# Layer 3 of a graph network: the edge products with W2 on two halves of TensorE, the bias written to PSUM ahead of them

## The chip, the cores and the metric

The kernel runs on one core of a Trainium2 chip. The metric is the device time of one execution in microseconds (us). The kernel before was run ten times: its median is 5800.87 us, the runs lie between 5796.89 and 5811.82 us. One further execution was recorded by the hardware profiler.

The engines are named as in the profile: PE is TensorE (PEld its weight loads), DVE is VectorE, ACT is ScalarE, POOL is GpSimd, SP is SyncE. A core's PSUM has eight banks of 128 partitions x 512 fp32 values.

## What is computed

Four graph layers over 8,192 nodes with 32 features and 262,144 edges sorted by destination; after each layer the node features are summed with the result and normalised. The change is in layer 3, where each edge has its own small weight matrices, made by a two-layer network from 32 edge features:

```python
h = relu(edge_feat @ W1 + b1)                      # 262144 x 64
w = (h @ W2 + b2).reshape(e, 4, 8, 8)              # 262144 x 256
s, v = node_attr[:, :8], node_attr[:, 8:].reshape(n, 8, 3)
m0 = 0.25 * (einsum(s[src]*sh0, w[:,0]) + C110 * einsum(v[src], sh1, w[:,3]))
m1 = 0.25 * (einsum(s[src], sh1, w[:,1]) + einsum(v[src]*sh0, w[:,2]))
out = segment_sum([m0, m1], dst) + self-interaction
x = layernorm(x + out)
```

`sh0` and `sh1` are the four values of `edge_attr_4`. All arithmetic is fp32.

## The kernel before

Layers 0 to 2 fill the first 3,180 us or so and are untouched. Layer 3 begins at line 1031 of `raw_layers`. It takes 512 edges at a time, four tiles of 128, called a **quad**; there are NQ = 512 quads, and two consecutive quads, q even and q + 1, are called a **pair** here (256 pairs).

Order is written out by hand. Each engine has a `Flow`: `after(marks)` makes the engine's queue wait for marks, `mark(ins)` gives one; every engine executes its instructions in the order in which the loop (lines 1162 to 1246) issues them. For iteration q that order is:

- `hidden(q + 2)`, for even q (lines 1139 to 1155): PE multiplies W1 with the edge features of two quads at once, on different 32-row and 64-column parts of the array, into the lower and upper 64 partitions of PSUM bank 2 (L1146). Then ACT makes relu with the bias b1 and moves each quad's 64x512 to SBUF `hs` (L1154), one instruction for a quad. There are four such buffers, each with a 65th row of ones, set once (L1067).
- the products with W2 (L1166 to 1172): four matmuls on PE, 65 rows x 128 edges against 65 rows x 256 columns; the 65th row of `w2_s` is b2, which the row of ones adds. They write two PSUM banks (3 and 4, or 5 and 6 in turn, `w_bank`). They wait for the quad's relu and for `w_free`, the mark of DVE's last read of these banks two quads earlier. Each fp32 matmul is two passes in the trace, so a quad has eight weight loads and eight matmuls.
- `fetch_rows(q + 8)` (L1089): POOL waits for the products of q, then issues four indirect gathers of 128 source rows each (L508, shown as L454, where the helper stands). So POOL may run eight quads ahead. Gathers are also limited to two groups of eight under way.
- the aggregation of quad q - 4 (L1179): a one-hot matrix against the message parts `p`, 344 columns, accumulated over a pair in bank 0 or 1. It waits for DVE's work on quad q - 2.
- on DVE: `factors` of the next pair (L1105 to 1117, waits for the pair's gathered rows), pieces of earlier quads (L1193, L1198), the one-hot matrix (L588), and then the products of the PSUM weights with the gathered values (L1207, L1210, three of L1214). The last of these is the mark `quad[q]["v"]` and `w_free`.
- on DVE, every second iteration: the sums of a finished pair (L1235 to L1238) into `win`.
- eight times in the layer, when a block of 1,024 nodes is complete (L1242): `windows` adds up the block's window sums on PE in the first half of a W2 bank (L575), and `normalize` runs on DVE with Square and Sqrt on ACT (L525 to L537, ACT at L532 and L534).

Edge features and `edge_attr_4` come by SP's queue, eight quads at a time, three buffers (`fetch`).

Of the kernel before, what the change touches and what calls it, by code (L numbers as in the profile page):

```python
# [15 lines left out]
AF = mybir.ActivationFunctionType  # L16
# [5 lines left out]
P = 128  # L22
N = 8192
E = 262144
D = 32
# [178 lines left out]
def raw_layers(tc, x, a, w0, w1, b1, w2, si, m, bad):  # L204
    nc = tc.nc
    PE, V, A, G, S = (Flow(tc, e, n) for e, n in ((nc.tensor, "pe"), (nc.vector, "dve"), (nc.scalar, "act"),
                                                  (nc.gpsimd, "pool"), (nc.sync, "sp")))
    bank, arena = m["bank"], m["arena"]
    x_a, x_b, src, row, rel = (m[k] for k in ("x_a", "x_b", "src", "row", "rel"))
    ident, shift, stack, small = (m[k] for k in ("ident", "shift", "stack", "small"))  # L210
# [40 lines left out]
    cut = Carve()  # L251
# [20 lines left out]
    cut = Carve(8192)  # L272
# [279 lines left out]
    def windows(c, acc, free):  # L552

        d0 = c * LC
        todo = []
        for j in [0, 1, 2, 3, -2, -1, 4]:
            lo, hi = 0, LC
            while 4 * (d0 + lo) + j < 0:
                lo += 1
            while 4 * (d0 + hi - 1) + j >= GG:  # L560
                hi -= 1
            if lo < hi:
                todo.append((j, lo, hi))
        nw = win.shape[1] // 4
        wv = win.rearrange("p (d j) f -> p d j f", j=4)
        PE.after(*free)
        pieces = []
        for j, lo, hi in todo:
            g0 = (4 * (d0 + lo) + j) // 4 % nw
            cutat = lo + min(hi - lo, nw - g0)  # L570
            pieces.append((j, lo, cutat, g0))
            if cutat < hi:
                pieces.append((j, cutat, hi, 0))
        for n, (j, lo, hi, g0) in enumerate(pieces):
            ins = PE.e.matmul(acc[:, lo * D:hi * D].rearrange("p (d f) -> p d f", f=D),  # L575
                              shift[:, P - WS * j:2 * P - WS * j], wv[:, g0:g0 + hi - lo, j % 4, :],
                              start=(n == 0), stop=(n == len(pieces) - 1))
        return PE.mark(ins)
# [457 lines left out]
    w1_s = cut(64)  # L1036
    b1_s = cut(1)
    w2_s = cut(256)
    hs = cut(4, 512)
    ef = cut(3, 2, 512)  # L1040
    sh = cut(3, WT, 4)
    a0 = cut(2, WT, 16)
# [19 lines left out]
        c_ld.add(S.e.dma_start(w1_s[q * D:(q + 1) * D, :], w1))  # L1062
    for h in range(2):
        c_ld.add(S.e.dma_start(b1_s[64 * h:64 * h + 64], b1))
    c_in = c_ld.add(S.e.dma_start(w2_s[0:65], w2))
    for k in range(4):
        hm = V.mark(V.e.memset(hs[64:65, k], 1.0))  # L1067

    e_ld = [Landing(tc, f"ld_ef{k}") for k in range(3)]
    s_ld = [Landing(tc, f"ld_sh{k}") for k in range(3)]  # L1070
# [50 lines left out]
    fetch(2)  # L1121
    PE.after(*free)
    A.after(*free)
    A.after(c_in, hm)

    h_free = None
    w_free = [zf[0], zf[1]]
# [11 lines left out]
    def hidden(q):  # L1139

        s = q // 8
        k = s % 3
        PE.after(batch[s]["e"], quad.get(q - 1, {}).get("h", h_free))
        for h in range(2):
            r = q % 4 + h
            ins = PE.e.matmul(bank[64 * h:64 * h + 64, 2, :], w1_s[r * D:(r + 1) * D, :],  # L1146
                              ef[r * D:(r + 1) * D, k, (q % 8) // 4, :], start=True, stop=True,
                              tile_position=(r * D, 64 * h))
        pm = PE.mark(ins)
        if q % 8 == 6:  # L1150
            ef_free[k] = pm
        for h in range(2):
            A.after(pm, quad.get(q + h - 4, {}).get("w"))
            quad[q + h] = dict(h=A.mark(A.e.activation(hs[0:64, (q + h) % 4], bank[64 * h:64 * h + 64, 2, :], AF.Relu,  # L1154
                                                       bias=b1_s[64 * h:64 * h + 64])))

    for q in range(AHEAD):
        fetch_rows(q)
    factors(0)
    PE.after(c_in, *zf)  # L1160
    hidden(0)
    for q in range(NQ + LAG3 + 2):

        if q % 2 == 0 and q + 2 < NQ:
            hidden(q + 2)
        if q < NQ:  # L1166
            k, wp = w_bank()
            PE.after(quad[q]["h"], w_free[k])
            for t in range(4):
                ins = PE.e.matmul(wp[:, t, :], hs[0:65, q % 4, t * P:(t + 1) * P], w2_s[0:65], start=True, stop=True)  # L1170
            quad[q]["w"] = PE.mark(ins)
            quad[q]["k"] = k, wp
            fetch_rows(q + AHEAD)
        c = q - LAG3
        if 0 <= c < NQ:
            g = c // 2
            PE.after(quad[c + 2]["v"], agg_free[g % 2] if c % 2 == 0 else None)
            for t in range(4):
                ins = PE.e.matmul(bank[:, g % 2, 0:MW], oh[:, c % NO, t, :], p[:, c % NP, t, :],  # L1179
                                  start=(c % 2 == 0 and t == 0), stop=(c % 2 == 1 and t == 3))  # L1180
            quad[c]["a"] = PE.mark(ins)

        prev = (V.sem, V.n)
        if q % 2 == 0 and q + 2 < NQ:
            factors(q // 2 + 1)
        V.after(prev)
        if q < NQ:
            V.after(factor[q // 2])
        V.after(quad.get(q - NP, {}).get("a"))
        ins = None  # L1190
        if 0 <= q - 2 < NQ:
            c = q - 2
            ins = V.e.tensor_tensor(p[:, c % NP, :, 320:344].rearrange("p t (o m) -> p t o m", m=3),  # L1193
                                    red[:, c % 2, :, :, None].to_broadcast([P, 4, 8, 3]),
                                    sh[:, (c // 8) % 3, (c % 8) * 4:(c % 8) * 4 + 4, None, 1:4].to_broadcast([P, 4, 8, 3]),
                                    op=OP.mult)
        if 0 <= q - 1 < NQ:
            ins = V.e.tensor_reduce(red[:, (q - 1) % 2], pr[:, (q - 1) % 2].rearrange("p t (o i) -> p t o i", i=8),  # L1198
                                    AX.X, OP.add)
        if q < NQ:  # L1200
            k, wp = quad[q]["k"]
            s, u = q // 8, (q // 8) % 2
            qs = slice((q % 8) * 4, (q % 8) * 4 + 4)
            pq = p[:, q % NP]
            one_hot(oh[:, q % NO], 4 * q, 4)
            V.after(quad[q]["w"])
            V.e.tensor_tensor(pr[:, q % 2].rearrange("p t (o i) -> p t o i", i=8),  # L1207
                              wp[:, :, 128:192].rearrange("p t (o i) -> p t o i", i=8),
                              xg[:, batch[s]["xg"], qs, None, 0:8].to_broadcast([P, 4, 8, 8]), op=OP.mult)
            V.e.tensor_tensor(pq[:, :, 0:128].rearrange("p t (o k) -> p t o k", k=16),  # L1210
                              wp[:, :, 0:128].rearrange("p t (o k) -> p t o k", k=16),
                              a0[:, u, qs, None, :].to_broadcast([P, 4, 8, 16]), op=OP.mult)
            for mm in range(3):
                ins = V.e.tensor_tensor(pq[:, :, 128 + 64 * mm:192 + 64 * mm].rearrange("p t (o i) -> p t o i", i=8),  # L1214
                                        wp[:, :, 192:256].rearrange("p t (o i) -> p t o i", i=8),
                                  vm[:, u, qs, mm, None, :].to_broadcast([P, 4, 8, 8]), op=OP.mult)
        if ins is not None:
            d = V.mark(ins)
            if q < NQ + 2:
                quad.setdefault(q, {})["v"] = d  # L1220
            if q < NQ:
                w_free[k] = d
                if 4 * (q + 1) % TP == 0:
                    taken[batch[s]["xg"]][4 * (q % 8) // TP] = d
            if 0 <= q - 2 < NQ and (q - 2) % 8 == 7:
                s = (q - 2) // 8
                sh_free[s % 3] = d
                if s + 3 < NS:
                    fetch(s + 3)

        c = q - LAG3 - 1
        if 0 <= c < NQ and c % 2 == 1:
            g = c // 2
            V.after(quad[c]["a"])
            V.e.tensor_reduce(win[:, g, 0:8], bank[:, g % 2, 0:128].rearrange("p (o k) -> p o k", k=16), AX.X, OP.add)  # L1235
            rm = V.mark(V.e.tensor_reduce(r1, bank[:, g % 2, 128:320].rearrange("p (mo i) -> p mo i", i=8), AX.X, OP.add))
            V.after(rm)
            gm = V.mark(V.e.tensor_tensor(win[:, g, 8:].rearrange("p (o m) -> p o m", m=3),  # L1238
                                          bank[:, g % 2, 320:344].rearrange("p (o m) -> p o m", m=3),
                                          r1.rearrange("p (m o) -> p o m", o=8), op=OP.add))  # L1240
            agg_free[g % 2] = gm
            while done < NB // LC and ready(done) <= g + 1:  # L1242
                k, wp = w_bank()
                acc = bank[:, 3 + 2 * k, 0:LC * D]
                w_free[k] = normalize(3, done, acc, windows(done, acc, (w_free[k], gm)), z, x_a)
                done += 1


# [469 lines left out]
```

## Time and profile before

| what | value |
|---|---|
| median of ten runs | 5800.87 us |
| the profiled execution, its time | 5800.9 us |
| the profiled execution, its span from first to last instruction | 5799.2 us |
| mean granted clock of PE | 0.885 |
| PE busy, matmuls | 4739.6 us, 82% of the span, 34,726 instructions |
| DVE busy | 4409.4 us, 76% |
| POOL busy | 4148.7 us, 72% |
| ACT busy | 1888.8 us, 33% |
| layer 3, 3183.00 to 5753.79 us: busy PE / DVE / ACT / POOL | 2468.12 / 2072.19 / 355.35 / 1947.70 of 2570.79 us |
| layer 3: granted clock | 0.96 |

The page of a profile gives, for each group of instructions, the line, the engine, the operation with its shapes and count, then "busy us, mean ns of one | idle time of the engine just before them, and what ended most of it". Matmuls are pipelined, so the mean duration of one is longer than the distance between two starts. The slices of the page are 40 equal parts of the span, some 145 us each; a digit is the busy share in tenths, and for PEclk the granted clock in tenths of full speed. A timeline row has the start and the length of a run of like instructions and how many they are.

### The profile page before, as it was taken

What the parts mean: (1) busy time and instruction counts of PE and PEld (TensorE: products, weight loads), DVE (VectorE), ACT (ScalarE), POOL (GpSimd) and SP (SyncE); (2) the same over time, 40 slices, a digit from 0 to 9 for tenths busy, and PEclk for the clock granted to TensorE, in tenths of its full rate; (3) what the DMA queues carried; (4) which work ended last, traced back from release to release, by engine and by line L of the source; (5) the groups of instructions that cost most, each with busy time, mean ns of one, the idle gap of its engine ahead of it and who ended that gap; (6) DMA issues with size and microseconds to landing.
All of it is one profiled execution on the core that took longest, in us unless ns stands there. A gap on an engine that the chain in (4) does not pass through costs nothing.

```text
span 5799.2 us, 89080 instructions
## 1 busy us (share of the span) xinstructions
PE 4739.6 (82%) x34726; PEld 3373.1 (58%) x34726; DVE 4409.4 (76%) x9512; ACT 1888.8 (33%) x3061; POOL 4148.7 (72%) x4238
## 2 busy tenths in 40 slices
PE   7456777768777788744499999999999999999998
PEld 3146666666666666522255666666666666666665
DVE  4269898989989898543356788878788878788786
ACT  5255555555555555200177111111111111111110
POOL 2677777777777777777356777777777777777775
PEclk7578888999899899756599899999999999999999
DMA  9636666769789799945576111111111111111111
GB/s 346 218 107 198 193 205 225 254 227 323 243 299 313 274 346 327 346 137 186 208 272 221 26 26 30 26 30 30 26 30 26 30 30 26 30 26 30 26 30 22
DMA packets 583102, 865.29 MB, mean 149 GB/s; under 512 B 102605, under 2 KB 441614, under 8 KB 549134
## 3 DMA queue, kind: packets, MB, share of 16 engines
q1 hardware_dynamic: 448094, 782.68, 38.2%
q0 software_dynamic: 134144, 73.67, 6.6%
q8 instruction: 275, 4.51, 0.3%
q10 hardware_dynamic: 432, 3.15, 0.2%
q14 instruction: 157, 1.29, 0.1%
HBM read 454.28 MB, written 404.88 MB: 148 GB/s over the span
## 4 chain that ended last, share of the span: by engine, by line
PE 27%; POOL 10%; DMA 6%; DVE 4%; issue 4%; ACT 0%; POOLq 0%; SPq 0%; DVEq 0%
PE bank L1179 11%; POOL f_arena L454 10%; PE bank L1170 9%; DMA f_arena<-fxtab,f_src 5%; PE bank L1009 4%; PE bank L1146 2%; PE bank L575 1%; DVE f_arena L1214 1%; DMA f_arena<-famat 1%; DVE f_arena L1210 0%; DVE f_arena L588 0%; PE bank L937 0%; PE bank L715 0%; DVE f_arena L1112 0%; DVE f_arena L1207 0%
## 5 line engine op out<-in xcount | busy, mean ns | idle before, releaser
L454 POOL DMA_INDIRECT f_arena<-fytab,f_row x2048 | 1960.5, 957 | 651.7 <-issue 542.2
L454 POOL DMA_INDIRECT f_arena<-fxtab,f_src x2048 | 1950.6, 952 | 643.4 <-issue 517.5
L654 PE MATMUL bank<-f_arena 64*128 64x128 f32 x16384 | 1207.6, 305 | 402.6 <-DVE f_arena L643 269.9
L654 PEld LDWEIGHTS bank<-f_arena 64*128 64x128 f32 x16384 | 1110.4, 211 | 483.6 <-DVE f_arena L643 296.1
L1179 PE MATMUL bank<-f_arena 128*128 128x344 f32 x4096 | 1313.0, 463 | 0.0
L1170 PE MATMUL bank<-f_arena 65*128 65x256 f32 x4096 | 1021.8, 393 | 70.3 <-DVE f_arena L1214 69.9
L1154 ACT ACTIVATE f_arena<-bank,f_arena 64x512 f32<-64x512 f32 x512 | 351.1, 686 | 2117.4 <-PE bank L1146 2110.9
L1170 PEld LDWEIGHTS bank<-f_arena 65*128 65x128 f32 x4096 | 770.1, 193 | 423.5 <-DVE f_arena L1214 142.1
L1179 PEld LDWEIGHTS bank<-f_arena 128*128 128x128 f32 x4096 | 800.0, 195 | 359.1 <-issue 31.7
L658 ACT ACTIVATE f_arena<-bank 128x512 uint8<-128x512 f32 x1024 | 612.9, 599 | 847.5 <-PE bank L654 723.7
L659 ACT ACTIVATE f_arena<-bank 128x512 f32<-128x512 f32 x1024 | 610.7, 596 | 0.0
L640 DVE TENSOR_TENSOR f_arena<-bank,f_arena 128x2048 f32<-128x2048 bf16 x256 | 586.6, 2291 | 8.7
L1214 DVE TENSOR_TENSOR f_arena<-bank,f_arena 128x256 f32<-128x256 f32 x1536 | 550.6, 413 | 0.0
L845 PE MATMUL bank<-f_arena 128*128 128x96 bf16 x2048 | 151.7, 225 | 325.2 <-DVE f_arena L811 325.0
L1110 DVE TENSOR_TENSOR f_arena<-f_arena 128x192 f32<-128x192 f32 x256 | 92.1, 360 | 399.0 <-DMA f_arena<-fxtab,f_src 397.3
L715 PE MATMUL bank<-f_arena,f_x_b 128*32 128x256 f32 x4096 | 312.7, 446 | 77.1 <-DMA f_arena<-famat 59.2
L588 DVE TENSOR_TENSOR f_arena<-bank,f_rel 128x512 f32<-128x512 f32 x512 | 348.6, 681 | 0.0
L1210 DVE TENSOR_TENSOR f_arena<-bank,f_arena 128x512 f32<-128x512 f32 x512 | 348.5, 681 | 0.0
L845 PEld LDWEIGHTS bank<-f_arena 128*128 128x128 bf16 x2048 | 110.4, 108 | 408.8 <-DVE f_arena L811 324.4
L638 DVE TENSOR_TENSOR f_arena<-bank,f_arena 128x1024 f32<-128x1024 bf16 x256 | 312.0, 1219 | 18.2 <-PE bank L654 16.0
L643 DVE TENSOR_TENSOR f_arena<-f_arena,bank 128x1024 f32<-128x1024 f32 x256 | 309.6, 1210 | 0.0
L965 POOL CAST f_arena<-f_arena 128x1536 bf16<-128x1536 uint8 x64 | 169.6, 2664 | 182.0 <-DMA f_arena<-fcmat 68.3
(146 smaller groups left out, 4404.8 us busy)
## 6 DMA issues: line engine op xcount, KB each, us to landing
famat<-f_arena SPq DMA_DIRECT2D x256, 1024.0 KB
f_arena<-famat SPq DMA_DIRECT2D x256, 1024.0 KB, 12.0
fytab<-f_arena SPq DMA_DIRECT2D x64, 1024.0 KB, 11.9
fcmat<-f_arena SPq DMA_DIRECT2D x256, 256.0 KB
f_arena<-fcmat SPq DMA_DIRECT2D x16, 4096.0 KB, 14.7
f_arena<-fytab,f_row POOLq DMA_INDIRECT x2048
f_arena<-fxtab,f_src POOLq DMA_INDIRECT x2048
f_arena<-laid_ea SPq DMA_DIRECT2D x64, 512.0 KB, 3.4
```

What stands on the lines that cost most here:

```text
L454: return G.e.indirect_dma_start(out=dest, out_offset=None, in_=table, in_offset=bass.IndirectOffsetOnAxis(ap=ix, axis=0))
L588: return V.e.tensor_tensor(o, iota[:, None, :].to_broadcast([P, n, P]), rel[:, t:t + n, None].to_broadcast([P, n, P]), op=OP.is_equal)
L640: V.e.tensor_tensor(oh_l[:, b], iota2[:, None, :, 0].to_broadcast([P, 16, P]), meta_l[:, pp, k0:k0 + 16, None].to_broadcast([P, 16, P]), o ...
L654: ins = PE.e.matmul(two[:, h].rearrange("p (c s j) -> p c s j", s=64, j=4)[:, :, :, j], oh_l[hs_, b, 4 * q + j, :], oh_k[hs_, b, 4 * q + j ...
L658: A.e.activation(st_c[:, b, q], two[:, :, 0:256], AF.Copy)
L659: pair_free[u] = am = A.mark(A.e.activation(st_a[:, b, :, q].rearrange("p z h w -> p h z w"), two[:, :, 256:512].rearrange("p h (z w) -> p ...
L715: ins = PE.e.matmul(acc[q * D:(q + 1) * D, :].rearrange("p (u h j) -> p u h j", h=2, j=4), x_b[:, 8 * z + s, :], mv[:, s], start=(first an ...
L1154: quad[q + h] = dict(h=A.mark(A.e.activation(hs[0:64, (q + h) % 4], bank[64 * h:64 * h + 64, 2, :], AF.Relu, bias=b1_s[64 * h:64 * h + 64])))
L1170: ins = PE.e.matmul(wp[:, t, :], hs[0:65, q % 4, t * P:(t + 1) * P], w2_s[0:65], start=True, stop=True)
L1179: ins = PE.e.matmul(bank[:, g % 2, 0:MW], oh[:, c % NO, t, :], p[:, c % NP, t, :], start=(c % 2 == 0 and t == 0), stop=(c % 2 == 1 and t = ...
L1210: V.e.tensor_tensor(pq[:, :, 0:128].rearrange("p t (o k) -> p t o k", k=16), wp[:, :, 0:128].rearrange("p t (o k) -> p t o k", k=16), a0[: ...
L1214: ins = V.e.tensor_tensor(pq[:, :, 128 + 64 * mm:192 + 64 * mm].rearrange("p t (o i) -> p t o i", i=8), wp[:, :, 192:256].rearrange("p t ( ...
```

## The change

The products use 64 rows instead of 65, and there are two sets side by side: the relu of a pair lies in one 128x512 buffer whose lower 64 partitions hold tiles 0 and 1 of both quads and whose upper 64 hold tiles 2 and 3. W2 is loaded to both halves of the partitions. A quad's four matmuls are issued in the order 0, 2, 1, 3, alternately on the lower and upper 64 rows of the array; tiles 0 and 1 write one bank, 2 and 3 the other. The edge features are laid out on the host to match.

The bias b2 is no longer a row of the product. It is loaded to all partitions (`b2_s`), and for each quad ACT copies it, four times over, to the quad's two PSUM banks before the products (new `biases`, 128x1024); the products then accumulate (`start=False`). The copy waits for `w_free`, the products wait for the copy. So that PSUM accumulates onto values that ACT wrote, the four banks are written once by PE at the layer's beginning (new `written`), and after each use by `windows`, the second half of that bank is written by PE again. Relu is one 128x512 instruction for a pair instead of two of 64x512, and `hs` has two buffers instead of four. In the program's order ACT gets the relu of q + 2 (for even q), then the bias copy of q, then that of q + 1.

```diff
-    hs = cut(4, 512)
+    b2_s = cut(256)
+    hs = cut(2, 512)
...
-    c_in = c_ld.add(S.e.dma_start(w2_s[0:65], w2))
-    for k in range(4):
-        hm = V.mark(V.e.memset(hs[64:65, k], 1.0))
+        c_ld.add(S.e.dma_start(w2_s[64 * h:64 * h + 64], w2[0:64, :]))
+    c_in = c_ld.add(S.e.dma_start(b2_s, w2[64:65, :].to_broadcast([P, 256])))
...
-        for h in range(2):
-            A.after(pm, quad.get(q + h - 4, {}).get("w"))
-            quad[q + h] = dict(h=A.mark(A.e.activation(hs[0:64, (q + h) % 4], bank[64 * h:64 * h + 64, 2, :], AF.Relu,
-                                                       bias=b1_s[64 * h:64 * h + 64])))
+        A.after(pm, quad.get(q - 3, {}).get("w"))
+        hm = A.mark(A.e.activation(hs[:, q // 2 % 2], bank[:, 2, :], AF.Relu, bias=b1_s))
+        quad[q] = dict(h=hm)
+        quad[q + 1] = dict(h=hm)
+
+    def written(b, c0):
+
+        return PE.e.matmul(bank[:, b, c0:512].rearrange("p (r c) -> p r c", c=256), ident,
+                           b2_s[:, None, :].to_broadcast([P, 2 - c0 // 256, 256]), start=(c0 == 0), stop=True,
+                           skip_group_check=True)
+
+    def biases(k, wp):
+
+        A.after(w_free[k])
+        return A.mark(A.e.activation(wp, b2_s[:, None, :].to_broadcast([P, 4, 256]), AF.Copy))
...
     hidden(0)
+    for b in range(3, 7):
+        ins = written(b, 0)
+    w_free[:] = [PE.mark(ins)] * 2
...
             k, wp = w_bank()
-            PE.after(quad[q]["h"], w_free[k])
-            for t in range(4):
-                ins = PE.e.matmul(wp[:, t, :], hs[0:65, q % 4, t * P:(t + 1) * P], w2_s[0:65], start=True, stop=True)
+            PE.after(quad[q]["h"], biases(k, wp))
+            for t in (0, 2, 1, 3):
+                hp, c0 = slice(32 * (t & 2), 32 * (t & 2) + 64), 256 * (q % 2) + t % 2 * P
+                ins = PE.e.matmul(wp[:, t, :], hs[hp, q // 2 % 2, c0:c0 + P], w2_s[hp], start=False, stop=True,
+                                  skip_group_check=True)
...
-                w_free[k] = normalize(3, done, acc, windows(done, acc, (w_free[k], gm)), z, x_a)
+                windows(done, acc, (w_free[k], gm))
+                w_free[k] = normalize(3, done, acc, PE.mark(written(3 + 2 * k, 256)), z, x_a)
...
-    laid["ea32"] = arrays["ea32"].reshape(P, 4, 512, D).transpose(1, 3, 0, 2).reshape(P, P, 512)
+    laid["ea32"] = arrays["ea32"].reshape(P, 2, 2, 2, 256, D).transpose(1, 3, 5, 0, 2, 4).reshape(P, P, 512)
```

## The prediction

> **What bounds the kernel now.** I read the page's table of slices first, then the groups by cost, then the waits of GpSimd (POOL) in layer 3, the stretch from 3183 to 5754 us that the change touches.
>
> ```profile
> PE   7456777768777788744499999999999999999998
> POOL 2677777777777777777356777777777777777775
> PEclk7578888999899899756599899999999999999999
> ...
> L454 POOL DMA_INDIRECT f_arena<-fxtab,f_src x2048 | 1950.6, 952 | 643.4 <-issue 517.5
> L654 PE MATMUL bank<-f_arena 64*128 64x128 f32 x16384 | 1207.6, 305 | 402.6 <-DVE f_arena L643 269.9
> L1179 PE MATMUL bank<-f_arena 128*128 128x344 f32 x4096 | 1313.0, 463 | 0.0
> L1170 PE MATMUL bank<-f_arena 65*128 65x256 f32 x4096 | 1021.8, 393 | 70.3 <-DVE f_arena L1214 69.9
> ```
>
> In slices 22 to 39 PE looks full (9) and POOL only 7 tenths busy. That misleads. The waits of POOL between 3183 and 5753 us tell it otherwise (line waited for; us, times, longest):
>
> ```profile
> POOL f_arena L454 <- issue: 516.9, 1696, 0.3
> POOL f_arena L454 <- DMA f_arena<-fxtab,f_src: 55.5, 182, 0.3
> ```
>
> No gap between two of the 2,048 gathers is over 0.3 us: POOL never waits for anybody, it issues without a break. In the timeline the first starts at 3179.33 and the last at 5752.85, lasting 0.94. That is 2574.5 us, or **10.06 us for a pair of quads** (256 pairs). VectorE (DVE) agrees: in layer 3 it waits 389.5 us at L1110 for gathered rows. PE is busy, but is it late? The timeline of the stage's end, where PE works without waiting (start, us, operation):
>
> ```profile
> 5757.17 1.89 PE L1170 MATMUL bank<-f_arena 65*128 65x256 f32 x8
> ...
> 5758.90 2.48 PE L1179 MATMUL bank<-f_arena 128*128 128x344 f32 x8
> ...
> 5761.22 1.89 PE L1170 MATMUL bank<-f_arena 65*128 65x256 f32 x8
> ```
>
> Start to start, a quad's W2 products take 1.73 and its aggregation (L1179) 2.32 us. Around `hidden` I use this stretch, PE and then ScalarE (ACT):
>
> ```profile
> 4504.70 1.07 PE L1146 MATMUL bank<-f_arena 32*64 32x512 f32 x4
> 4505.71 1.99 PE L1170 MATMUL bank<-f_arena 65*128 65x256 f32 x8
> 4507.54 1.32 PE L1179 MATMUL bank<-f_arena 128*128 128x344 f32 x4
> ```
> ```profile
> 4505.83 1.40 ACT L1154 ACTIVATE f_arena<-bank,f_arena 64x512 f32<-64x512 f32 x2 [7.91 <-PE bank L1146]
> ```
>
> Hidden to products 1.01, products to aggregation 1.83; aggregation to hidden is 2.42 elsewhere (5740.30 to 5742.72). PE's pair: 2.42 + 1.01 + 1.83 + 2.32 + 1.73 = 9.31 us, 0.75 under POOL's 10.06. So the gathers bound layer 3 and PE is a close second.
>
> **The change, part by part.** Sums go against the profiled execution, 5800.9 us (span 5799.2 and 1.7 around it); the median shown is 5800.87, the same.
>
> *Products in halves.* 8 passes of 256 columns at 0.216 (1.73 / 8) become 4 steps of two passes side by side, if the halves overlap. L654 has just that shape, 64 rows on each half: 16,384 passes of 128 columns keep PE busy for 1207.6 us, 74 ns each, or 148 for 256 columns, where L1170 has 1021.8 / 4096 = 249. L654's share includes low clock; in its bursts at full clock two passes start together every 0.112 us. So 4 x 0.216 = 0.87 us for a quad where nothing precedes it, instead of 1.73; bounds 0.87 and 1.73 (no overlap). I take 0.87. By itself this frees 1.7 us of a pair on an engine that was not the bound: worth nothing.
>
> *Changes of array shape.* Before: aggregation to hidden (2.42 - 2.32 = 0.10) and hidden to products (1.01 - 4 x 512 columns two at a time, 0.86 = 0.15). After, products to aggregation and back are changes too: three more of 0.10 to 0.20 in a pair (two to an odd quad's products and back, one behind the even quad's). I take 0.15. The Trainium skill ("TensorEngine Tiling (Array Packing)", Key Properties) says that a change of tiling mode drains TensorE; without any such cost the pair's sum below would be 9.48.
>
> *Relu of two quads at once.* L1154's two of 0.70 (1.40 / 2) become one over 128 partitions, 0.70: half a relu less for ACT, which was waiting anyway.
>
> *Bias first, and where it queues.* This decides. Each quad gets a 128x1024 copy on ACT into PSUM. No row has SBUF to PSUM; bounds: L481, 128x1024 from PSUM, 1.03 us; L532 (SBUF, 128x256, 0.41) and L659 (128x512, 0.60) bound the slope and give 0.96 to 1.1. I take 1.03. Two make 2.1 us of ACT's idle 8.7 in a pair: no load problem. But the order is: PE runs `hidden(q+2)`, then the products of q, which wait for the bias of q. ACT has relu of q+2 **ahead of** that bias, and that relu waits for the very `hidden(q+2)` PE has just issued. PE cannot go on: hidden ends, 0.05 (L1146's end to L1154's start), relu 0.70, bias 1.03, 0.05 back: **1.83 us in which PE stands, once a pair**. Behind the waiting products on PE's queue lie the aggregation of q-4, the next products, and with them VectorE's turn and POOL's gather for q+8 (L1092). The odd quad's bias follows at once on ACT and hides beside 0.97 + 2.32 us of PE.
>
> PE's pair at full clock: 2.42 + 1.07 (hidden to its end) + 1.83 + 0.97 (0.10 to load the first weights) + 2.32 + 0.87 = 9.48, and 3 x 0.15 = **9.93** (9.78 to 10.08), against POOL's 10.06. The halves give back what the wait takes.
>
> *Clock.* A gap of 1.83 us is not only 1.83 us. The granted clock moves in steps of 3.41 us. Four such steps now (us; busy PE, PEld, DVE, ACT, POOL; granted clock; DMA):
>
> ```profile
> 4096.45:4099.87 3.42, 2.73 (x10) 0.97 (x9) 2.64 (x10) 0.64 (x1) 2.51 (x4) 1.00 0.12 27
> 4099.87:4103.28 3.41, 1.71 (x8) 1.53 (x9) 3.34 (x11) 0.73 (x2) 2.49 (x4) 1.00 0.06 12
> 4103.28:4106.69 3.41, 3.41 (x8) 2.12 (x7) 3.20 (x11) 0.00 (x0) 2.79 (x3) 0.50 0.08 14
> 4106.69:4110.11 3.42, 3.42 (x15) 2.58 (x15) 3.42 (x11) 0.00 (x0) 2.52 (x3) 1.00 0.09 19
> ```
>
> PE idle for 1.7 of 3.41 us, and the next step is at half clock: 8 instructions where 15 fit. Over all steps of layer 3: at full clock and under 60% busy, 28 of 28 were followed by half clock; at 60 to 85%, 8 of 23; above, none. There were 32 spells of half clock with 51 steps, 1.6 steps or 5.4 us each, and every return followed a step at least 90% busy. A gap of 1.83 lies within one step in (3.41 - 1.83) / 3.41 = 46% of pairs (busy 46%); when split, one part exceeds 1.37 (busy under 60%) in half of the rest, 27%. That is 73% certain falls and part of the remainder: I take 0.85 spells for a pair, each losing half of 5.4 us: 0.85 x 2.7 = 2.3 us. Bounds: 0.5 spells of one step (0.85 us) and 0.95 of two steps (3.2 us).
>
> The Trainium skill ("TensorE: Matmul & The Clock Gate", Part 1) has the clock fall back only after an idle window of about 3.4 us. By that rule a gap of 1.83 us never costs clock, and the sum would be the second case below; the steps above, with half a window idle, say otherwise.
>
> *Normalisation blocks.* Seven times inside the stage ACT's Square and Sqrt (L532, L534) wait for VectorE, now with the next quad's bias behind them. In the block at 3557.92 the window sums held PE to 3563.81; Sqrt ended at 3566.89, so with bias and 0.05 the products start at 3567.97: 4.2 us later, about 10 us of PE a block. Before, the 0.75 us a pair over 32 pairs swallowed 5.9; now nothing does: +70. The constants' extra loads and four first writes lie beside the first pair's gathers (10 us): nothing. At the end, shorter products spare up to 1.5 us before the last aggregations.
>
> **Sum.** 9.93 + 2.3 = 12.2 us a pair; 256 x (12.2 - 10.06) = +548; blocks +70; less some 14 us by which rows are gathered early (eight quads, 40.2 us, less the 26 that issue, landing and the turn of a pair use). 5800.9 + 604 = 6405, **6400 us**. With the bounds 10.63 to 13.3: 6000 to 6690.
>
> **Rivals.** *Wait without clock loss:* 9.93 at full clock regains 0.13 x 32 = 4 of a block's 10 us; 7 x 6 - 14 = +28, 5829; at 10.08, 5862; some falls reach 6000. For: PE has less to do. Against: the 28 of 28.
>
> *The gathers still carry it (not slower):* if PE's whole pair, clock and all, stays under 10.06 - 10 / 32 = 9.75 us, POOL's unbroken 10.06 sets the time and only the end's 1.5 us goes: 5799. For: POOL's waits now. Against: 9.78 is already my lowest sum. POOL's floor also forbids more: faster than that by 0.2% has no source I can find.
>
> *The halves do not overlap:* 9.93 + 2 x 0.87 = 11.7, with clock 14.0 us: 256 x 3.9 + 56 = 6850. Against: L654.
>
> **How the numbers follow.** Forecast case 70%, its range 6000 to 6690; wait without much clock loss 11% (5820 to 6000); gathers carry it 10% (5799, counted as within 0.2%, 11.6 us, about what can be told from no change); no overlap 7% (6850); faster 2%. The range 5820 to 6690 leaves out the last three. Slower 88%, same 10%, faster 2%.
>
> **What would show it.** Right: PE's products idle some 1.8 us once a pair, released by the bias copy; half-clock slices through layer 3; gathers with gaps over 0.3 us released by the products; VectorE waiting for PE instead of rows. The halves: product passes starting in twos. Wrong: a clock row still at 9 (then 5829 to 5862), or POOL still without a gap (then 5799), or a bias copy far from 1.03 us.

## The result, and the profile after

The changed kernel takes 5923.16 us (median of 8 runs, 5917.63 to 5926.21) against 5802.33 us for the kernel before on the same chips (28 runs). The ratio is 1.0206, 95% interval [1.0197, 1.0215]: slower by 121 us. The forecast was 6400 us with a range from 5820 to 6690; so the direction and the range hold, but the loss is a fifth of the one forecast. The profiled execution spans 5919.6 us.

The lines of the page that answer to those of before (a product is now L1185, an aggregation L1195; L1166 is the bias copy and L1153 the relu):

```profile
PE   7456777777787788642898888888888888888887
POOL 2677777777777777777166777767677776767674
PEclk7578898989898898665698999999999999999999
...
L454 POOL DMA_INDIRECT f_arena<-fxtab,f_src x2048 | 1939.5, 947 | 752.1 <-issue 563.8
...
L1195 PE MATMUL bank<-f_arena 128*128 128x344 f32 x4096 | 1364.8, 476 | 0.0
...
L1185 PE MATMUL bank<-f_arena 64*128 64x256 f32 x4096 | 634.5, 431 | 467.6 <-ACT bank L1166 467.6
...
L1166 ACT ACTIVATE bank<-f_arena 128x1024 f32<-128x1024 f32 x512 | 505.1, 1021 | 15.1 <-DVE f_arena L1230 15.1
```

Three things are to be seen. The products keep PE busy for 634.5 us instead of 1021.8: the halves do work side by side. PE now stands idle ahead of them for 467.6 us, and what ends the wait is the bias copy. And the clock row still shows nines through layer 3, where the forecast wanted half-clock slices.

POOL, which never waited before, now does (its waits in layer 3; us, times, longest):

```profile
POOL f_arena L454 <- issue: 563.8, 1850, 0.3
POOL f_arena L454 <- PE bank L1185: 154.6, 150, 7.5
```

So PE's loop sets the time. Here is the wait in it, first PE, then ACT:

```profile
4704.64 1.07 PE L1146 MATMUL bank<-f_arena 32*64 32x512 f32 x4
4707.42 0.80 PE L1185 MATMUL bank<-f_arena 64*128 64x256 f32 x2 [1.71 <-ACT bank L1166]
```
```profile
4705.76 0.69 ACT L1153 ACTIVATE f_arena<-bank,f_arena 128x512 f32<-128x512 f32 x1 [7.39 <-PE bank L1146]
4706.34 1.97 ACT L1166 ACTIVATE bank<-f_arena 128x1024 f32<-128x1024 f32 x2
```

`hidden` ends at 4705.71, relu and the first bias copy follow on ACT, and the products start at 4707.42: 1.71 us in which PE stands, in every pair.

I took the time from one `hidden` to the next for all 255 intervals of the trace. 201 of them take 9.945 us, but for four at the beginning. 47 take 1.55 us longer, and those are the ones in which the clock was halved for one step. Seven, with a normalisation block, take 10.38 us longer. 255 x 9.945 + 47 x 1.55 + 7 x 10.38 = 2681, against 2679.7 measured from the first to the last, and 2567.8 before. Of the 120.4 us between the two spans these are 112.0; 4.7 lie ahead of the layer (its first gather starts at 3184.07 instead of 3179.33; in the runs below it lies anywhere from 3176 to 3189, and the layers ahead are the same in all, so this is scatter), and 3.5 lie between the first gather and the first `hidden`, which waits there for edge features that are queued behind the constants: the last of the constants lands 5.0 us after its issue, before 2.1.

### The profile page after: what moved, and what is told of

It reads as the page before. It is cut to its first block, busy times and chain, and to the rows that moved or that the text cites. A ratio compares the mean times of both kernels' runs of the same rounds, so it can differ in the third digit from the quotient of the medians.

```text
span 5919.6 us, 89562 instructions
## 1 busy us (share of the span) xinstructions
PE 4495.3 (76%) x34750; PEld 2946.0 (50%) x34750; DVE 4421.5 (75%) x9508; ACT 2190.3 (37%) x3317; POOL 4133.2 (70%) x4238
## 4 chain that ended last, share of the span: by engine, by line
PE 43%; ACT 7%; DVE 1%; issue 1%; POOL 1%; DMA 0%; SPq 0%; DVEq 0%
PE bank L1195 22%; PE bank L1185 10%; PE bank L1146 4%; ACT bank L1166 4%; PE bank L1009 4%; ACT f_arena L1153 3%; PE bank L715 1%; PE bank L937 1%; PE bank L575 1%; POOL f_arena L454 1%; DMA f_arena<-famat 0%; SPq L906 0%; ACT f_arena L965 0%; DVE f_arena L1230 0%; DVE f_lnf L530 0%
## 5 line engine op out<-in xcount | busy, mean ns | idle before, releaser
L1195 PE MATMUL bank<-f_arena 128*128 128x344 f32 x4096 | 1364.8, 476 | 0.0
L654 PEld LDWEIGHTS bank<-f_arena 64*128 64x128 f32 x16384 | 1108.6, 211 | 479.5 <-DVE f_arena L643 297.1
L1195 PEld LDWEIGHTS bank<-f_arena 128*128 128x128 f32 x4096 | 759.2, 196 | 513.2 <-issue 213.8
L1185 PE MATMUL bank<-f_arena 64*128 64x256 f32 x4096 | 634.5, 431 | 467.6 <-ACT bank L1166 467.6
L1153 ACT ACTIVATE f_arena<-bank,f_arena 128x512 f32<-128x512 f32 x256 | 176.2, 688 | 1953.1 <-PE bank L1146 1953.1
L1185 PEld LDWEIGHTS bank<-f_arena 64*128 64x128 f32 x4096 | 379.9, 200 | 846.2 <-ACT bank L1166 696.8
L1223 DVE TENSOR_TENSOR f_arena<-bank,f_arena 128x256 f32<-128x256 f32 x512 | 215.2, 420 | 479.3 <-PE bank L1185 479.2
L1230 DVE TENSOR_TENSOR f_arena<-bank,f_arena 128x256 f32<-128x256 f32 x1536 | 550.7, 414 | 0.0
L1166 ACT ACTIVATE bank<-f_arena 128x1024 f32<-128x1024 f32 x512 | 505.1, 1021 | 15.1 <-DVE f_arena L1230 15.1
```

What stands on the lines that cost most here:

```text
L654: ins = PE.e.matmul(two[:, h].rearrange("p (c s j) -> p c s j", s=64, j=4)[:, :, :, j], oh_l[hs_, b, 4 * q + j, :], oh_k[hs_, b, 4 * q + j ...
L1153: hm = A.mark(A.e.activation(hs[:, q // 2 % 2], bank[:, 2, :], AF.Relu, bias=b1_s))
L1166: return A.mark(A.e.activation(wp, b2_s[:, None, :].to_broadcast([P, 4, 256]), AF.Copy))
L1185: ins = PE.e.matmul(wp[:, t, :], hs[hp, q // 2 % 2, c0:c0 + P], w2_s[hp], start=False, stop=True, skip_group_check=True)
```

## What the prediction left open

Two questions follow. Is it really the order on ACT, and nothing else in the change, that costs the time? And why does the clock fall in 47 pairs and not in 0.85 x 256 = 218?

The theory for the second was formed from the changed kernel's trace. The granted clock moves in steps of 3.413 us in every trace here, and the loop's turns do not shift them. A pair of 9.945 us is 0.295 us short of three steps (10.24). So the gap of 1.71 us moves by 0.295 us a pair against the steps. When nearly all of it lies in one step, the next step runs at half clock, that pair takes 1.55 us more, and this pushes the gap onto the boundary of two steps, where it does no harm. It needs 1.55 / 0.295 = 5.25 pairs to come back: 255 / 5.25 = 49 falls, where 47 are seen. Two places in the changed kernel fit it. First a gap within a step, then one on a boundary; each row is a step (us; busy PE, PEld, DVE, ACT, POOL; granted clock; DMA):

```profile
3976.73:3980.15 3.42, 1.87 (x7) 0.41 (x6) 2.92 (x10) 1.50 (x2) 2.54 (x3) 1.00 0.06 14
3980.15:3983.56 3.41, 3.25 (x10) 2.02 (x11) 1.12 (x3) 1.05 (x2) 2.13 (x3) 0.50 0.07 10
3983.56:3986.97 3.41, 3.41 (x17) 2.01 (x16) 3.11 (x11) 0.00 (x0) 2.50 (x4) 1.00 0.07 13
```
```profile
4058.65:4062.07 3.42, 2.56 (x10) 0.90 (x8) 3.39 (x12) 0.81 (x2) 2.51 (x4) 1.00 0.09 14
4062.07:4065.48 3.41, 2.56 (x13) 1.74 (x14) 1.60 (x5) 1.74 (x2) 2.77 (x3) 1.00 0.10 19
4065.48:4068.89 3.41, 3.41 (x17) 1.99 (x16) 3.34 (x11) 0.00 (x0) 2.53 (x3) 1.00 0.08 14
```

In the first, PE is idle for 1.55 us of one step and the next is at 0.50, for a single step. In the second the same 1.71 us are split, 0.86 and 0.85, and the clock stays at 1.00. The rivals are that the clock plays no part, and that falls come by chance, in one pair of five.

## The experiments

**The bias copy ahead of the relu.**

```diff
+        if q < NQ:
+            k, wp = w_bank()
+            bm = biases(k, wp)
         if q % 2 == 0 and q + 2 < NQ:
             hidden(q + 2)
         if q < NQ:
-            k, wp = w_bank()
-            PE.after(quad[q]["h"], biases(k, wp))
+            PE.after(quad[q]["h"], bm)
```

> The changed kernel with one move: on ACT the bias copy of quad q is issued ahead of the relu that follows hidden(q+2); all work and all shapes stay. Theory (the order on ACT makes PE stand once a pair): PE's pair falls from 9.95 by the gap of 1.7 us to about 8.2 us, the gathers at 10.06 a pair bound the layer again, no gather waits for the products, time 5798 to 5802 us. Rival (the new shapes, the bias copies themselves or the first write of the banks cost the time, wherever they stand in the queue): 5880 us or more.

Measured: 5798.72 us, ratio 0.9997 [0.9988, 1.0006]. The longest wait of POOL is 0.3 us again:

```profile
POOL f_arena L454 <- issue: 521.7, 1712, 0.3
POOL f_arena L454 <- DMA f_arena<-fxtab,f_src: 49.7, 163, 0.3
```

A pair without other waits takes PE 8.17 us. All 121 us hang on the order of two instructions on ACT; the shapes, the copies and the first writes cost no time as long as the gathers set it. This kernel has 68 spells of half clock in the layer, more than the changed one, and they cost nothing: PE is 1.9 us a pair ahead.

**The gap filled with idle work.** Three matmuls that nobody reads, behind `hidden`; in a second run one (`range(1)`):

```diff
             hidden(q + 2)
+            if q >= LAG3:
+                u = (q - LAG3) // 2 % 2
+                PE.after(agg_free[u])
+                for _ in range(3):
+                    PE.e.matmul(bank[:, u, 0:256], ident, shift[:, 0:256], start=True, stop=True)
```

> The changed kernel with three idle 256-column matmuls behind hidden(q+2) on PE, into a bank that PE overwrites next; nothing reads them. They leave some 0.3 of the 1.71 us gap, while the products still start when the bias is written. Theory (the gap costs its own length, and on top the clock, in those pairs only where nearly all of the gap lies in one step of 3.41 us): no step at half clock between the blocks, pairs stay at 9.95, and the time is 5833 us (7 blocks x (10.35 - 32 x 0.11) - 14 above before), 5825 to 5850. Rival A (the clock plays no part): 5923. Rival B (time is lost to PE being late with more work, as the prediction's sum per pair would say for any PE work): above 5923.

Measured: 5846.62 us, 1.0079 [1.0063, 1.0094]. With 3 x 512 columns of work more in a pair, the kernel is 77 us faster than the changed one. The products still start when the bias is there, after 0.21 us of idleness (L1184 is the filling):

```profile
4713.55 1.07 PE L1146 MATMUL bank<-f_arena 32*64 32x512 f32 x4
4714.56 1.56 PE L1184 MATMUL bank<-f_shift,f_ident 128*128 128x256 f32 x6
4716.33 1.13 PE L1190 MATMUL bank<-f_arena 64*128 64x256 f32 x8 [0.21 <-ACT bank L1166]
```

A pair takes 9.945 us as before; outside the blocks only two pairs show a fall. So the gap's own length and the blocks cost some 45 of the 121 us, and the clock the rest. Rivals A (5923) and B (above it) are out.

> As with three, but one idle matmul: about 1.1 to 1.2 us of the gap stay, a step is then at least 65% busy. Theory from the changed kernel's steps (busy up to 58% falls, above does not): no falls between blocks, 5833 us as with three. Rival from the steps of before (60 to 85% busy: 8 of 23 fell): falls stay at one pair in five or more, 5900 us or more.

Measured: 5858.38 us, 1.0095 [1.0080, 1.0111]. With 1.08 us of the gap left, eight pairs outside the blocks still fall. It lies near the forecast of the theory and far from 5900, but "no falls" was too strong: of 161 steps with 65 to 70% busy, six were followed by half clock.

**Longer pairs.** One idle matmul of 175 columns behind each pair's second aggregation (the gap stays at 1.71 us), and in a later run four of 320:

```diff
             quad[c]["a"] = PE.mark(ins)
+            if c % 2 == 1:
+                PE.after(agg_free[1 - g % 2])
+                PE.e.matmul(bank[:, 1 - g % 2, 0:175], ident, shift[:, 0:175], start=True, stop=True)
```

> The changed kernel with one idle 175-column matmul behind each pair's second aggregation: 0.29 us more PE work in a pair, so 9.95 becomes 10.24 us, three steps of the clock (3 x 3.413); the gap of 1.71 us stays. Theory (the gap drifts by 0.30 us a pair against the clock's steps, a fall comes when it lies in one step, and a fall pushes it 1.5 us on to a boundary): at 10.24 it no longer drifts, a fall or two after each block and then none, under 25 falls instead of 56, and the time is 5800 + 256 x 0.18 + 7 x 10.35 - 14 = 5905 us, 5895 to 5925, though PE has 75 us more to do. Rival (falls come by chance, one pair in five): 5923 + 75 = 5998 us.

Measured: 5922.03 us, 1.0209 [1.0194, 1.0225]: 75 us of work more, and the same time as the changed kernel. The starts of `hidden` stand 10.24 us apart, three steps, and ten spells of half clock are left instead of 55:

```profile
4037.20 1.07 PE L1146 MATMUL bank<-f_arena 32*64 32x512 f32 x4
...
4047.45 1.07 PE L1146 MATMUL bank<-f_arena 32*64 32x512 f32 x4
...
4057.69 1.07 PE L1146 MATMUL bank<-f_arena 32*64 32x512 f32 x4
```

It is some 17 us above the 5905 worked out (at the edge of the range given). Chance falls (5998) are out. But the theory's reason, a gap that rests on a boundary, is not the whole of it: in 63 steps of this run PE is only 50 to 55% busy, and one of them is followed by half clock. The last section says what tells these apart.

> The changed kernel with four idle 320-column matmuls behind each pair's second aggregation: 2.16 us more PE work, 9.95 becomes 12.10 us at full clock. A fall adds 1.55, and 12.10 + 1.55 = 13.65 is four of the clock's steps. Theory (the gap's place in the steps decides): once the gap lies in a step it stays there, nearly every pair falls, some 230 falls or more, a pair takes 13.65, and the time is 5801 + 256 x (13.65 - 10.06) + 58 = 6780 us, 6700 to 6800. Without the clock: 6380. With one fall in five pairs: 6460. It is the counterpart of the run with 0.29 us more, where the same rule makes the falls vanish.

Measured: 6783.93 us, 1.1693 [1.1673, 1.1712]. Now every pair falls: 258 spells, one step each, and the pair is four steps long where the gap has settled:

```profile
4019.92 1.07 PE L1146 MATMUL bank<-f_arena 32*64 32x512 f32 x4
...
4033.57 1.07 PE L1146 MATMUL bank<-f_arena 32*64 32x512 f32 x4
...
4047.23 1.07 PE L1146 MATMUL bank<-f_arena 32*64 32x512 f32 x4
```

**The halves made serial by order (did not do what it was to do).** `for t in (0, 1, 2, 3)` instead of `(0, 2, 1, 3)`:

> The changed kernel with the four matmuls of a quad issued 0, 1, 2, 3 instead of 0, 2, 1, 3: two on the lower half and then two on the upper, so that the halves no longer work side by side; all else stays. A quad's products go from 0.87 towards 1.73 us, a pair from 9.95 to about 11.67 at full clock. Without the clock: 5801 + 256 x 1.61 + 7 x 10.35 - 14 = 6271 us. Theory with the clock: at 11.67 (10.24 + 1.43) a fall of 1.5 us pushes the gap of 1.71 us by 2.98, nearly one whole step, so most pairs fall, some 4 in 5 or 200 in all: 6271 + 200 x 1.55 = 6580 us, 6500 to 6620. Rival (one pair in five falls, as in the changed kernel): 6271 + 80 = 6350 us. The prediction's own account (0.85 spells of 5.4 us) gave 6850.

Measured: 5924.06 us, 1.0205 [1.0188, 1.0222], as the changed kernel. The order makes no difference: the passes still start in twos, and the group is as cheap as before:

```profile
L1185 PE MATMUL bank<-f_arena 64*128 64x256 f32 x4096 | 633.1, 429 | 466.2 <-ACT bank L1166 466.2
```

So this run, and the next with the same order and the bias copy first, say nothing of products that run one after the other.

> The bias copy ahead of the relu, and the halves not side by side (order 0, 1, 2, 3): PE's pair 8.2 + 1.7 = 9.9 us without a gap. Theory (gathers bound the layer at 10.06, the halves' overlap is worth nothing as long as PE stays below): 5800 us, up to 5825 if a block's 10 us is not made up in 32 pairs of 0.16. Rival (the overlap of the halves carries the result of the reordered kernel): 5900 or more.

Measured: 5804.53 us, 1.0000 [0.9990, 1.0010].

**No halves.** W2 twice in SBUF, padded with zeros to 128 rows:

```diff
-                hp, c0 = slice(32 * (t & 2), 32 * (t & 2) + 64), 256 * (q % 2) + t % 2 * P
-                ins = PE.e.matmul(wp[:, t, :], hs[hp, q // 2 % 2, c0:c0 + P], w2_s[hp], start=False, stop=True,
+                c0 = 256 * (q % 2) + t % 2 * P
+                ins = PE.e.matmul(wp[:, t, :], hs[:, q // 2 % 2, c0:c0 + P], w2_s[:, t // 2], start=False, stop=True,
```

> The changed kernel without the halves: W2 stands twice in SBUF with zeros on the other 64 partitions, and a quad's four matmuls use all 128 rows, so that nothing runs side by side and the array keeps its shape from the products to the aggregation. Bias copies, relu and all waits stay. A pair at full clock: 2.78 (hidden to products) + 1.83 + 2.32 + 1.73 + 2.42 = 11.08 us. Theory with the clock: a pair now moves the gap of 1.71 us by 0.84 us against the clock's steps, a fall moves it by 1.55 more; followed by hand, about one pair in two falls: 5801 + 256 x (11.08 + 0.74 - 10.06) + 58 = 6310 us, 6250 to 6350, some 120 falls. Without the clock: 6120. With one fall in five pairs: 6200. With the prediction's 0.85 spells of 5.4 us: 6710.

Measured: 6329.53 us, 1.0912 [1.0894, 1.0930]. A pair takes 11.08 us at full clock, as worked out, and there are 124 spells of half clock, where some 120 were expected. In the trace a pair with a fall (12.77 us) and one without (11.08) take turns. Without the halves the change costs 530 us (against the 5799.99 us of the kernel before in the same session) instead of 121: the difference is what the halves give back.

> The same products on 128 rows, with the bias copy ahead of the relu: 11.08 - 1.71 = 9.37 us of PE in a pair, as in the kernel before, and no halves at all. Theory (gathers bound the layer at 10.06; the halves' 1.7 us are worth nothing there): 5800 us, 5795 to 5815. Rival (only the halves keep the bias copies from costing time): 5840 or more.

Measured: 5802.67 us, 1.0002 [0.9992, 1.0011]. With the bias copy first, the halves take nothing off the time.

**Half of the gathers left out**, in the kernel before and in the one with the bias copy first, to see what the gathers hide:

```diff
-            indirect(xg[:, k, t, :], table[:, :], ix[:, s * WT + t:s * WT + t + 1]).then_inc(ld.sem, 16)
-            ld.n += 16
+            if t % every == 0:
+                indirect(xg[:, k, t, :], table[:, :], ix[:, s * WT + t:s * WT + t + 1]).then_inc(ld.sem, 16)
+                ld.n += 16
...
-            rows[q // 2] = gathers(xtab, src, q // 8, q % 8 * 4, 4)
+            rows[q // 2] = gathers(xtab, src, q // 8, q % 8 * 4, 4, 2)
```

> The kernel before with every second gather of layer 3 left out (tiles 1 and 3 of each quad keep old rows in SBUF; part of the computation is left out): POOL's floor drops from 10.06 to about 5 us a pair. Theory (PE is the next bound at 9.31 a pair, full clock since it has no gaps): 5801 - 256 x 0.75 + 7 blocks of 6 = 5650 us, 5630 to 5680. Rival (VectorE is next, 8.14 a pair): 5350 to 5450.

Measured: 5636.59 us, 0.9710 [0.9694, 0.9727].

> The reordered kernel (bias copy ahead of the relu) with the same gathers left out. Theory (the halves are a true gain of 1.1 us a pair on PE that the gathers hide): PE at 8.17 and VectorE at 8.14 a pair, 5801 - 256 x 1.85 + 7 blocks of 10 = 5400 us, 5380 to 5480, some 230 below the kernel before with the same gathers left out. Rival (the changed kernel's new waits or changes of array shape eat the gain even without gathers): within 60 us of that kernel.

Measured: 5396.51 us, 0.9297 [0.9282, 0.9313]: 240 us less than the kernel before with the same gathers left out (230 were expected): a pair without other waits takes 8.17 us here and 9.30 there. The halves are a real gain of PE time. In the full kernel the gathers, at 10.06 us a pair, hide all of it.

No kernel that computes everything beats the one before: with the bias copy first it is equal, and POOL issues its gathers without a break in both.

## Why the prediction was right, and where it was wrong

- **What bounds the kernel: right.** Every reordered version comes back to 5799 to 5805 us, and with half of the gathers left out both kernels become faster.
- **The halves overlap: right.** 634.5 us of busy time for the products; between aggregations a quad's products take 1.07 us with their changes of array shape.
- **Changes of array shape: right in kind, somewhat small.** Products to aggregation 1.07 us (0.97 without a cost, 0.10 more), aggregation to products 2.52 (0.20 more), odd products 1.07 (0.20 more), and aggregation to `hidden` 2.52 instead of the 2.42 of before (0.10 more, not taken into the sum): 0.6 in a pair, 0.45 taken.
- **The wait on ACT's order: right in place and nearly in size.** 1.71 us, 1.83 forecast. ACT starts the bias copy 0.58 us after the relu's start, although the relu is shown with 0.69; I had taken 0.70. The copy takes 1.02, 1.03 taken.
- **PE's pair at full clock: right, partly by luck.** 9.945 us, 9.93 forecast: the changes of shape cost 0.14 more than taken, the wait is 0.12 shorter.
- **The blocks: right.** 10.38 us each, 10 taken.
- **The credit of 14 us for rows gathered early: wrong.** From the last `hidden` to the end it is 47.4 us now and was 47.2 before, so nothing was saved there; and the constants' loads, which I took for nothing, put the first `hidden` 3.5 us later behind the first gather.
- **The clock: the step that failed.** "I take 0.85 spells for a pair, each losing half of 5.4 us: 0.85 x 2.7 = 2.3 us." Measured: 47 spells in 255 pairs, 0.18, of 1.55 us each, **0.29 us a pair**. That is 73 us instead of the 589 of 256 x 2.3; with the credit that did not come, it accounts for all but some 20 us of the difference between 5923 and the 6405 of the sum.

Both factors were too large. The length came from the spells of before; here 49 of 55 spells end after one step (61 steps in all). Of the 14 steps of before that were followed by a further one at half clock, PE stood idle for over a fifth in 5, but was busy for 93% or more in the other 9; why these did not bring the clock back stays open. The frequency was wrong twice. The 46% for a gap within one step was about right as a share of all places where a gap can begin: a gap of 1.71 us brings the half clock from 47% of them (1.59 of 3.41 us, last section). The step from there to 0.85 added split gaps, by the busy shares seen before; in the runs a gap that begins in the other 53% costs no clock, however it is split. And the prediction took the gap's place in the steps as random from pair to pair. It is not: the loop is nearly three steps long, and each fall moves the gap to where it costs nothing, so that 0.18 is left. The two runs with longer pairs show it on both sides of the truth: the same gap of 1.71 us costs hardly any clock at 10.24 us a pair, and one fall in every pair at 12.10. The rule that idle PE time costs clock was right and was needed: without it the forecast for the changed kernel would have been 5829 to 5862, as the filled gap measures (5847), and the kernel takes 5923.

A range that reached from 5820 to 6690 said that this term was uncertain; its bounds (0.85 to 3.2 us a pair) still did not include 0.29, and it was the other case, wait without much clock loss, given 11%, that held the time. The range held by luck, not by the forecast's own sum.

Two counts of the prediction do not come out of the trace again. In layer 3 of the kernel before I count 23 of 23 steps under 60% busy at full clock that were followed by half clock (28 of 28 in the prediction), and 31 spells of 45 steps that begin in it (32 of 51), 1.45 steps or 5.0 us each. With that length the forecast would have been some 50 us lower.

The page "TensorE: Matmul & The Clock Gate" of the Trainium skill, Part 1, describes a free-running window of 3413 ns. The steps of 3.413 us here agree, and that the window does not follow the kernel is the very thing my sum had left out. The same part lets the clock fall back after an idle window; the steps above, 1.55 of 3.42 us idle, again do not agree.

## What to carry to other kernels

When an instruction is added to a queue, write down what stands ahead of it there and what that one waits for: here a copy that was ready to run stood behind a relu that waited for the work PE had just begun, and moving the copy ahead of it gave back all 121 us. A gain on an engine that isn't the bound is spent by the first wait that makes it the bound. And a short gap that returns in every turn of a loop must be laid against the clock's fixed steps with the loop's own length; one fall changes where the next gap lies.

## What the hardware showed that was not expected

- The order in which four matmuls on the two halves of the array are issued made no difference (5924.06 and 5923.16 us): with two lower ones ahead of two upper ones, eight passes in all, the starts still come in twos 13 ns apart, 0.2 to 0.3 us from one two to the next.
- The busy share of a step does not alone decide whether the clock falls. At 50 to 55% busy, 156 of 157 steps were followed by half clock in the run with pairs of 12.10 us, and 1 of 63 in that with 10.24. Here is a step of each and the one behind it, first at 10.24, then at 12.10:

```profile
4110.10:4113.52 3.42, 1.84 (x11) 1.27 (x12) 1.84 (x6) 2.47 (x3) 2.31 (x3) 1.00 0.09 14
4113.52:4116.93 3.41, 3.41 (x17) 2.03 (x16) 3.34 (x11) 0.00 (x0) 2.49 (x4) 1.00 0.05 10
```
```profile
4101.08:4104.49 3.41, 1.83 (x8) 0.43 (x6) 0.53 (x1) 1.53 (x2) 1.62 (x2) 1.00 0.09 14
4104.49:4107.90 3.41, 3.28 (x10) 2.02 (x11) 1.16 (x3) 1.02 (x2) 0.92 (x1) 0.50 0.03 5
```

- What tells the two apart, for gaps of one length, is where the gap begins. The five kernels with the wait of 1.71 us unfilled (the changed one, the other order, both with longer pairs, and the one without halves) have 1,255 such gaps (1.68 to 1.75 us, from 3225 us on, begun in a step at full clock). All 470 that begin 0.39 to 1.98 us into their step are followed by half clock, and none of the other 785. A gap that begins in the first 1.70 us lies wholly in its step; the range seen is nearly as wide, but lies 0.3 to 0.4 us later. What is counted in a step, and why the range lies later, is not shown.
- More work on PE made the kernel faster: three idle matmuls in the gap, 77 us.
